# Two-layer graph network on one core: products of seven for the queries, one pass over the adjacency, softmax sums through DRAM

## The chip, the cores and the metric

The kernel runs on one core of a Trainium2 chip. The metric is the device time of one execution in microseconds (us). A core has five engines that work side by side, each on its own queue of instructions, in order: TensorE (PE, matrix products), VectorE (DVE), ScalarE (ACT), GpSimd (POOL) and SyncE (SP). SP and POOL also issue the DMA transfers here. An instruction that depends on another engine or on a transfer waits at the head of its queue, and what stands behind it waits too. SBUF is the on-chip memory of 128 partitions; PSUM holds the results of PE.

## The reference

The input is x (16 graphs, 1024 nodes, 256 channels) and one adjacency matrix of 1024 x 1024 that all graphs share. Two layers are computed, each with a layer norm before and the input added after.

```python
# layer 0
h = jnp.maximum(_layernorm(x), 0.0)          # per graph: fea = h transposed
c_adj = jnp.mean(fea, axis=1)                # one number per node
A = jnp.abs(jnp.abs(sigmoid(diff) - 0.5) - 0.5) * 2.0   # diff: c_adj of all pairs of nodes
Wg = adj * A_s                               # A_s: the symmetric mean of A
g = relu(einsum('bcn,bnm->bcm', fea, Wg) * para)        # the queries, 4 heads of 64
k, v = h @ kv_w
out = softmax(q k^T * scale) v               # attention over all 1024 nodes
# layer 1
A_norm = adj + I; deg = column sums + row sums - diagonal; dinv = rsqrt(deg)
agg = einsum('nm,bmd->bnd', A_norm * dinv[:, None] * dinv[None, :], h1)
out = bn(relu(bn(agg @ W1.T + b1)) @ W2.T + b2)         # bn: statistics over all nodes of all graphs
```

Everything is in 32-bit floats. Two things matter for the change. The weights Wg of the queries differ from graph to graph and have to be made anew for each. The matrix of the second layer is the same for all graphs and is scaled on both sides by dinv, the inverse root of the degrees.

## The kernel before

The first layer and the first product of the second run in `layers()`, graph after graph; the rest of the second layer (`second()`) follows once the statistics over all graphs are known. Profile lines written as L149 are line numbers of the kernel before.

**Attention.** `attention()` runs 256 steps: 16 graphs, two pairs of heads (k), two halves of 512 queries (f), four groups g of two node tiles. A step issues the scores of its group on PE (`sc`, L704), their exponentials on ACT (`p`, L712) and the additions of these on DVE (`acc`, L734), and then the product with the values of the step before (`o`, L745). After the four groups of a unit, `divide()` sums `acc` over the partitions with a product by ones (`sums`, L762). The result is 64 times repeated in each head's partitions, a tile of 128 x 512; DVE takes its reciprocal in four parts (`inv`, L771), multiplies `os` by it (L774), PE transposes (`ot`, L798) and DVE adds to x (L802). Two reductions (L777, L778) keep the extremes of `inv` in `seen` for a check at the end, which decides whether a slower variant of the kernel (`shifted`) has to run.

**Background.** PE is kept busy between scores by pieces of other work, each of eight matmuls of 512 columns. `background(b)` is a generator of these pieces, and a running sum of their costs (`due`, `done`) decides how many follow in each step. While graph b is in attention, its pieces are: the queries of graph b+1 (`queries`, `pg`, 16 pieces), the keys and values of b+1 (`keys_values`, `pk` and `pv`), the aggregation of b-1 over the adjacency (`aggregate`, `pa`, 14 pieces), the first linear product of b-1 (`hidden`, `py`), and the preparation of b+2. `weave` puts side work of the other engines between the pieces: `weigh` makes the weights `w` of the queries (ACT makes abs and tanh, L394 and L402; DVE multiplies by the loaded adjacency, L381), `Norm` makes the layer norms.

**Seven products.** `aggregate` already computes its 1024 x 1024 by 1024 x 256 product in the Strassen-Winograd way: the matrices are cut into quarters, seven products of quarters replace eight, and the quarters are combined by additions before and after. The combined quarters of the adjacency do not depend on the graph. `graph()` makes them once, during graph 1: it loads tiles `au`, scales them by the row `dbc` of dinv (L239), combines them on POOL (L246 to L249), and stores seven matrices in DRAM (`aht_d`, L251 to L253), from which SP loads pieces for each graph (`aht`). The degrees come before that, during graph 0: `degrees()` loads the transposed adjacency a first time (`at`), sums its rows on ACT, and takes the diagonal on DVE.

**Buffers.** Tiles come from pools that hand out their buffers in turn: a new tile waits until the last reader of the tile that had its buffer is done. `p4` has four buffers for each tag; the adjacency (`adj`, `at`, `au`, `aht`) shares one tag there, and `w` has another. `py` holds `y` and the small combined tiles. The order of the instructions on each engine is that in which the program issues them.

**The second layer.** `hidden` stores its results with POOL (`y_d`, L565). `second()` loads them again with SP (`yin_f`, L973), applies the statistics that POOL and DVE finish (`sm`, L82, L83, L917 to L919), combines the quarters of `w2` on POOL (L963 to L966) and multiplies (`m_f`, L1017).

Of the kernel before, what the change touches and what calls it, by code (L numbers as in the profile page):

```python
# [23 lines left out]
def gnn_two_layers_kernel(  # L24
# [36 lines left out]
    w2 = const.tile([P, HC, C], F32, name="w2")  # L61
# [4 lines left out]
    stats2 = const.tile([P, CC, B * NH, 6], F32, name="stats2")  # L66
# [6 lines left out]


# [10 lines left out]
    def layers(shifted):  # L85
# [12 lines left out]
        p3 = st.enter_context(tc.tile_pool(name=f"p3_{kind}", bufs=3))  # L98
        p4 = st.enter_context(tc.tile_pool(name=f"p4_{kind}", bufs=4))
# [41 lines left out]

        def bank(name):
            return ps_mm.tile([P, FB], F32, tag="mm", name=name)
# [15 lines left out]
        def load_adj(q, th, name):  # L159
            t = p4.tile([P, TH, FB], F32, tag="adj", name=name)  # L160
            nc.sync.dma_start(
                out=t,
                in_=adj[th * TH * P : (th + 1) * TH * P, q * FB : (q + 1) * FB].rearrange(
                    "(t p) m -> p t m", p=P
                ),
            )
            return t
# [4 lines left out]
        dbc = big.tile([P, N], F32, name="dbc")  # L172
        w1 = big.tile([P, CC, H1], F32, name="w1")
        rows = big.tile([P, NH, NT], F32, name="rows")

        def columns_of(col, name):

            cbs = []
            for g in range(NT // 4):
                cb = p2.tile([P, 4, P], F32, tag="cb", name=f"cb_{name}_{g}")  # L180
                nc.vector.tensor_copy(
                    cb, col[:, 4 * g : 4 * g + 4].unsqueeze(2).to_broadcast([P, 4, P])
                )
                cbs.append(cb)
            return cbs
# [9 lines left out]
        def load_adj_t(t, name):  # L195
            tile_ = p4.tile([P, N], F32, tag="adj", name=f"{name}_{t}")
# [3 lines left out]
        deg_sm = big.tile([P, 6, NT], F32, name="deg")  # L200
        row, diag, col, deg, tmp_deg, dinv = (deg_sm[:, i, :] for i in range(6))

        def degrees():

            nc.sync.dma_start(out=w1, in_=w1_t.rearrange("(k p) j -> p k j", p=P))
            nc.sync.dma_start(out=w2, in_=w2_t.rearrange("(k p) c -> p k c", p=P))
            nc.vector.tensor_reduce(row, rows.rearrange("p q t -> p t q"), AX.X, ALU.add)
            for t in range(NT):
                a = load_adj_t(t, "at")
                yield 0.0  # L210
                blk = a[:, t * P : (t + 1) * P]
                nc.scalar.activation(a, a, AF.Copy, accum_out=col[:, t : t + 1])
                db = p1.tile([P, P], F32, tag="db", name=f"db_{t}")
                nc.vector.tensor_mul(db, blk, ident)
                nc.vector.tensor_reduce(diag[:, t : t + 1], db, AX.X, ALU.add)
                yield 0.0
            nc.vector.tensor_add(deg, col, row)
            nc.vector.tensor_sub(deg, deg, diag)
            rsqrt(dinv, deg, 1.0, tmp_deg)

        def graph():


            HT, HB = NT // 2, FB // 2
            for t in range(HT):
                for part in range(2):
                    cols = slice(part * HB, (part + 1) * HB)
                    a = p4.tile([P, 2, NH, HB], F32, tag="adj", name=f"au_{t}_{part}")
# [6 lines left out]
                    for n in range(2):  # L235
                        if part == t * P // HB:
                            blk = a[:, n, n, t * P % HB : t * P % HB + P]
                            nc.vector.tensor_add(blk, blk, ident)
                        nc.vector.tensor_mul(  # L239
                            a[:, n], a[:, n], dbc.rearrange("p (m c) -> p m c", m=NH)[:, :, cols]  # L240
                        )
# [12 lines left out]
                    yield 0.0  # L254

# [107 lines left out]
        def weigh(b):  # L363
# [11 lines left out]
            for slot in range(2 * NH * NP + 1):  # L375
# [11 lines left out]
                if not odd and i < NH * NP:  # L387
# [3 lines left out]
                    w = p4.tile([P, TH, FB], F32, tag="w", name=f"w_{b}_{q}_{th}")  # L391
# [14 lines left out]

        def queries(b):

# [65 lines left out]
        def quarters(b):  # L474


            h = hs["b", b]
            HT = NT // 2
            return [h[:, n * HT : (n + 1) * HT, c * P : (c + 1) * P] for c in (0, 1) for n in (0, 1)]

        def combine(b):


            a11, a12, a21, a22 = quarters(b)
            s1s[b] = p1.tile([P, NT // 2, P], F32, tag="s1", name=f"s1_{b}")
            nc.vector.tensor_add(s1s[b], a21, a22)
            nc.vector.tensor_sub(a21, a11, a21)

        def aggregate(b):
# [5 lines left out]
            def load(upto):  # L495
                while len(pieces) <= min(upto, 7 * NP // 2 - 1):
                    i, th = divmod(len(pieces), NP // 2)
                    i = order[i]
                    a = p4.tile([P, TH, FB], F32, tag="adj", name=f"aht_{b}_{i}_{th}")
# [3 lines left out]
            load(2)  # L503
            yield 0.0
            a11, a12, a21, a22 = quarters(b)
            s1 = s1s[b]
# [4 lines left out]
            add, sub = nc.vector.tensor_add, nc.vector.tensor_sub  # L511

# [4 lines left out]
            def second(m):  # L517
                add(c11, m, c12)
                sub(a12, a12, a11)

            def fifth(m):
                add(c22, m, c21)
                add(c12, m, c12)

            for i, (left, after) in enumerate(
# [6 lines left out]
                    (a22, lambda m: add(c21, m, c21)),  # L532
                    (a12, lambda m: add(c12, m, c12)),
# [3 lines left out]
                for th in range(NP // 2):  # L537
                    n = i * NP // 2 + th
                    load(n + 3)
# [35 lines left out]
        def normed(b):  # L575
# [3 lines left out]
            combine(b)  # L579
# [4 lines left out]
        def normed_last():  # L584
# [6 lines left out]
            combine(B - 1)  # L591
            nc.gpsimd.dma_start(out=x1_d[B - 1], in_=xs[B - 1])

        def prepare(b, products):
# [8 lines left out]
            for k in range(CC):  # L603
                yield from weave(islice(products, 3), (0, islice(w, 3)))
# [7 lines left out]
        def background(b):  # L612

            nothing = iter(())
            if b == 0:
                yield from prepare(1, nothing)
                yield from weave(queries(1), (0, weighers[1]), (1, degrees()))
                cbs = columns_of(dinv, "deg")
                if B > 2:
                    load_x(2)  # L620
                    yield from weave(keys_values(1), (1, Norm(2, True).all()))
                else:
                    yield from keys_values(1)
# [3 lines left out]
                if B > 2:  # L627
                    yield from prepare(2, nothing)
# [3 lines left out]
            if b + 1 < B:  # L632
                whole = graph() if b == 1 else nothing
                yield from weave(queries(b + 1), (0, weighers[b + 1]), (0, whole))
                yield next(gather)
                yield from weave(keys_values(b + 1), (0, normed(b - 1)))
# [79 lines left out]
        class Unit:  # L716


            def __init__(self, b, k, f):
                self.at = (b, k, f)  # L720
                self.name = f"{b}_{k}_{f}"
                self.acc = None
                self.later = []
# [32 lines left out]
            def divide(self):  # L756

                b, k, f = self.at
                self.pt = ps_t.tile([P, FB], F32, tag="t", name=f"sums_{self.name}")
                for e in range(2):  # L760
                    r = slice(e * HD, (e + 1) * HD)
                    nc.tensor.matmul(  # L762
                        self.pt[r, :], ones, self.acc[:, e, :], start=True, stop=True
                    )
                self.inv = p1.tile([P, FB], F32, tag="inv", name=f"inv_{self.name}")
                u = (b * CC + k) * NH + f

                def invert(half):
                    for j in range(2 * half, 2 * half + 2):
                        c = slice(j * P, (j + 1) * P)  # L770
                        nc.vector.reciprocal(self.inv[:, c], self.pt[:, c])  # L771

                def scale():
                    nc.vector.tensor_mul(self.os, self.os, self.inv)  # L774

                def watch():
                    nc.vector.tensor_reduce(seen[:, 0, u : u + 1], self.inv, AX.X, ALU.max)  # L777
                    nc.vector.tensor_reduce(seen[:, 1, u : u + 1], self.inv, AX.X, ALU.min)  # L778

                invert(0)  # L780
                self.later = [lambda: invert(1), scale]
                self.watch = watch

            def behind_piece(self):
                if self.later:
                    self.later.pop(0)()

            def behind_pieces(self):
                while self.later:
                    self.behind_piece()  # L790

            def finish(self):
# [4 lines left out]
                for j in range(J):  # L797
                    nc.tensor.transpose(  # L798
                        pt[:, j * P : (j + 1) * P], self.os[:, j * P : (j + 1) * P], ident
                    )  # L800
                dst = xs[b][:, f * J : (f + 1) * J, k * P : (k + 1) * P]
                nc.vector.tensor_add(dst, pt.rearrange("p (j c) -> p j c", c=P), dst)  # L802
# [3 lines left out]
        def attention():  # L806
# [7 lines left out]
            for s in range(len(steps) + 2):  # L814
                if s < len(steps):
                    unit, g = steps[s]
                    b = unit.at[0]
                    if s % per_graph == 0:
# [3 lines left out]
                        total = 41.0 * (b + 1 < B) + 24.0 * (b > 0) + 6.0 * (b + 2 < B)  # L822
# [7 lines left out]
                finished = ended = None  # L830
                if pending and pending[0][1] <= s:
                    finished, _ = pending.pop(0)
                    finished.finish()
                if top:
                    done += advance(bg)
                    top = False
                if s < len(steps):
                    for pr in made:
                        unit.add(pr)
                if before is not None:  # L840
                    (last, g_last), prs = before
                    last.values(g_last, prs)
                    if g_last == NG - 1:
                        last.divide()
                        ended = last


                        pending.append((last, s + (2 if last.at[0] < B - 1 else 1)))
                while done < due and not top:
# [7 lines left out]
                    if ended is not None and cost > 1.0:  # L857
                        ended.behind_piece()
                if ended is not None:
                    ended.behind_pieces()  # L860
                if finished is not None:
                    finished.watch()
# [3 lines left out]
        with st:  # L866
            if shifted:
                for b in range(B):
# [7 lines left out]
                    run(weave(queries(b), (0, weighers[b])))  # L876
# [333 lines left out]
```

## Time and profile before

| | |
|---|---|
| median of 3 runs | 2698.32 us (2697.36 to 2698.34) |
| profiled execution, its own time | 2699.94 us |
| span of the profile | 2698.1 us |
| PE busy | 2620.7 us |
| DVE busy | 1742.3 us |
| ACT busy | 1292.3 us |
| POOL busy | 363.2 us |
| DMA | 355.05 MB, mean 132 GB/s |

Busy time counts what an engine executes, waits left out; matmuls overlap, so a busy PE says that the next matmul was there, not that the array was full. In the rows of groups, a form like `128x512 f32<-128x512 f32 x64 | 43.9, 686 | 3.3` gives the sizes, the count, the total busy time in us, the mean of one in ns, and the idle time just before, with the engine or transfer that ended it. A graph in the middle of the first layer takes 151 us.

### The profile page before, as it was taken

The page shows a single profiled execution, that of the slowest core. Times are in us where ns is not written, and L with a number is a line of the kernel's source. Part 1 is how long each engine was busy: PE and PEld are TensorE (multiplying, and loading weights), DVE is VectorE, ACT ScalarE, POOL GpSimd, SP SyncE. Part 2 cuts the span into 40 slices and gives each one's busy share as a digit, 9 for nine tenths or more (in the row PEclk, how much of TensorE's full clock was granted, in tenths as well). Part 3 has the DMA queues.
Part 4 walks back from the last instruction along what each step waited for, and adds up shares of the span by engine and source line. Part 5 has one row for each costly group of instructions (what it writes and reads, how often), then busy time and mean ns, then how long its engine had stood idle before and what let it go on. Part 6 is the DMA issues. An engine that isn't in the chain of part 4 may idle for free.

```text
span 2698.1 us, 32021 instructions
## 1 busy us (share of the span) xinstructions
PE 2620.7 (97%) x12106; PEld 968.3 (36%) x12106; DVE 1742.3 (65%) x2624; ACT 1292.3 (48%) x1845; POOL 363.2 (13%) x428
## 2 busy tenths in 40 slices
PE   7999999999999999999999999999999999989994
PEld 3333333333333333333333333333333333324443
DVE  5767666666666656666666666566666666656675
ACT  5653444536363544445363635444453634335544
POOL 0016000000000100000000001000000001026653
PEclk9999999999999999999999999999999999999997
DMA  4416414243332424142423324241424213355549
GB/s 156 159 58 225 161 53 164 86 148 103 107 116 98 141 80 158 51 168 83 150 100 109 114 98 141 84 155 51 168 82 152 99 63 118 113 215 187 202 182 364
DMA packets 128613, 355.05 MB, mean 132 GB/s; under 512 B 11969, under 2 KB 32961, under 8 KB 122305
## 3 DMA queue, kind: packets, MB, share of 16 engines
q1 hardware_dynamic: 109120, 278.44, 30.3%
q0 software_dynamic: 19328, 74.46, 7.3%
q8 instruction: 98, 1.61, 0.2%
q14 instruction: 67, 0.54, 0.1%
HBM read 278.41 MB, written 74.45 MB: 131 GB/s over the span
## 4 chain that ended last, share of the span: by engine, by line
PE 93%; DMA 3%; DVE 2%; issue 2%; ACT 1%; POOL 0%; SPq 0%; POOLq 0%; DVEq 0%; ACTq 0%
PE sc L704 18%; PE o L745 18%; PE pg L149 16%; PE pa L149 13%; PE py L149 7%; PE m_f L1017 7%; PE pk L149 4%; PE pv L149 4%; PE sums L762 2%; DMA out_dram<-xo_f 2%; PE ot L798 1%; PE htp L352 1%; PE cbp_c L192 1%; DMA y_d<-y 0%; DVE acc L734 0%
## 5 line engine op out<-in xcount | busy, mean ns | idle before, releaser
L712 ACT ACTIVATE p<-sc 128x1024 f32<-128x1024 f32 x512 | 496.4, 1021 | 700.8 <-PE sc L704 700.6
L734 DVE TENSOR_TENSOR acc<-acc,p 128x1024 f32<-128x1024 f32 x384 | 471.2, 1227 | 133.8 <-ACT p L712 112.5
L704 PE MATMUL sc<-q,k 64*128 64x512 f32 x2048 | 510.6, 617 | 0.5 <-ACT p L712 0.5
L745 PE MATMUL o<-p,v 128*64 128x512 f32 x2048 | 496.1, 605 | 0.0
L149 PE MATMUL pg<-w,h_a 128*64 128x512 f32 x2048 | 457.1, 596 | 7.5 <-DVE q L432 7.5
L149 PE MATMUL pa<-aht,h_b 128*64 128x512 f32 x1536 | 346.0, 592 | 2.7 <-DMA aht<-aht_d 2.7
L704 PEld LDWEIGHTS sc<-q,k 64*128 64x128 f32 x2048 | 176.6, 186 | 321.9 <-issue 270.3
L149 PEld LDWEIGHTS pg<-w,h_a 128*64 128x64 f32 x2048 | 148.2, 138 | 301.8 <-issue 281.7
L771 DVE RECIPROCAL inv<-sums 128x128 f32<-128x128 f32 x256 | 223.7, 921 | 24.6 <-PE sums L762 24.6
L149 PE MATMUL py<-at,w 128*64 128x512 f32 x1024 | 230.8, 592 | 2.1 <-ACT y L564 2.1
L745 PEld LDWEIGHTS o<-p,v 128*64 128x64 f32 x2048 | 124.3, 136 | 286.1 <-issue 285.9
L394 ACT ACTIVATE w<-cbc,csum 128x512 f32<-128x512 f32 x256 | 170.2, 714 | 74.3 <-PE pg L149 74.2
L731 DVE TENSOR_TENSOR acc<-p,p 128x1024 f32<-128x1024 f32 x64 | 78.5, 1226 | 194.8 <-ACT p L712 194.8
L381 DVE SCALAR_TENSOR_TENSOR w<-w,adj 128x1024 f32<-128x1024 f32 x128 | 156.5, 1223 | 54.7 <-ACT w L402 54.7
L149 PEld LDWEIGHTS pa<-aht,h_b 128*64 128x64 f32 x1536 | 110.6, 137 | 216.6 <-issue 204.9
L564 ACT ACTIVATE y<-py,vec 128x512 f32<-128x512 f32 x128 | 87.6, 684 | 188.4 <-PE py L149 155.1
L565 POOL DMA_DIRECT2D y_d<-y x128 | 70.7, 553 | 685.1 <-ACT y L564 681.9
L402 ACT ACTIVATE w<-w 128x1024 f32<-128x1024 f32 x128 | 134.8, 1053 | 1.7
L149 PEld LDWEIGHTS py<-at,w 128*64 128x64 f32 x1024 | 74.0, 137 | 147.8 <-issue 131.3
L149 PE MATMUL pv<-kvw,ht 128*64 128x256 f32 x1024 | 116.2, 379 | 0.4 <-DVE v L469 0.4
L82 POOL TENSOR_SCALAR lnsm_b<-mv_b 128x4 f32<-128x4 f32 x32 | 7.3, 230 | 805.2 <-DVE mv_b L277 805.1
L802 DVE TENSOR_TENSOR x<-ot,x 128x512 f32<-128x512 f32 x64 | 44.2, 691 | 110.6 <-PE ot L798 109.8
(133 smaller groups left out, 2526.4 us busy)
## 6 DMA issues: line engine op xcount, KB each, us to landing
aht<-aht_d SPq DMA_DIRECT2D x224, 512.0 KB, 4.2
adj<-in_adj_dram SPq DMA_DIRECT2D x128, 512.0 KB, 4.2
y_d<-y POOLq DMA_DIRECT2D x128, 256.0 KB, 2.8
yin_f<-y_d SPq DMA_DIRECT2D x32, 1024.0 KB, 6.3
x<-in_x_dram SPq DMA_DIRECT2D x32, 512.0 KB, 4.7
para<-in_para_dram SPq DMA_DIRECT2D x64, 256.0 KB, 4.1
x_d<-x POOLq DMA_DIRECT2D x16, 1024.0 KB, 4.2
xo_f<-x_d SPq DMA_DIRECT2D x32, 512.0 KB, 8.5
```

Of the source, the lines that this page charges most:

```text
L149: nc.tensor.matmul(dst[r], left[:, r], right, start=start, stop=stop)
L381: nc.vector.scalar_tensor_tensor(w, w, 1.0, a, op0=ALU.add, op1=ALU.mult)
L394: nc.scalar.activation(w[:, t, :], cbc[:, q * FB : (q + 1) * FB], AF.Abs, bias=csum[:, th * TH + t : th * TH + t + 1], scale=-1.0,)
L402: nc.scalar.activation(made[i], made[i], AF.Tanh, scale=-0.5 / C)
L564: nc.scalar.activation(y, made, AF.Identity, bias=b1[:, j : j + 1])
L704: nc.tensor.matmul(sc[:, e, :], ks[b][k][r, m * P : (m + 1) * P], qs[b][k][r, f * FB : (f + 1) * FB], start=True, stop=True,)
L712: nc.scalar.activation(pr, sc, AF.Exp)
L731: nc.vector.tensor_add(self.acc, self.held, pr)
L734: nc.vector.tensor_add(self.acc, self.acc, pr)
L745: nc.tensor.matmul(self.o[r, :], vs[b][k][:, m, r], pr[:, e, :], start=(m == 0), stop=(m == NT - 1),)
L771: nc.vector.reciprocal(self.inv[:, c], self.pt[:, c])
L1017: nc.tensor.matmul(made, left[:, j, :], right[:, j, :], start=(j == 0), stop=(j == JH - 1))
```

## The change

- From graph 2 on, `queries` uses seven products of quarters, 14 pieces instead of 16. Left operands are quarters of h, right operands quarters of the weights, which DVE turns into differences (`take`) in place; nine additions from PSUM put the four results together. Graphs 0 and 1 keep the old form, now `plain_queries`. Eight buffers hold `w` (pool `p8`, which `aggregate`'s loads share, five ahead instead of three).
- `degrees()` and `graph()` become one pass during graph 0: each `au` tile is loaded once, summed on ACT, its diagonal taken on DVE, combined on POOL without the scale and stored. `aggregate` multiplies its results by `dbc` instead (`scale`). The tiles of the adjacency have three buffers instead of four.
- The sums of exponentials: `sums()` copies the product by ones from PSUM (ACT), writes one row of each head to DRAM, and reads it back transposed as 128 x 8 (three DMAs on POOL). `add_output()` takes the reciprocal of this small tile and applies it after the transposes. The unit is finished two steps after its last group, in the last graph too, except for the last two units.
- The keys of b+1 come before its queries, the norm of b-1 begins within the queries, x of graph 2 is loaded earlier.
- `w2` is loaded, and `stats2` allocated, in the pools of the second layer.

The diff, cut to its core:

```diff
-    w2 = const.tile([P, HC, C], F32, name="w2")
+    sums_d = [dram.tile([2, FB], F32, name=f"sums_d{u}") for u in range(B * CC * NH)]
+        p8 = st.enter_context(tc.tile_pool(name=f"p8_{kind}", bufs=8))
+        def double(slots):
+            for _ in slots:
+                next(slots, None)
+                yield 0.0
...
-            t = p4.tile([P, TH, FB], F32, tag="adj", name=name)
+            t = p3.tile([P, TH, FB], F32, tag="adj", name=name)
...
-            nc.sync.dma_start(out=w2, in_=w2_t.rearrange("(k p) c -> p k c", p=P))
...
-                    a = p4.tile([P, 2, NH, HB], F32, tag="adj", name=f"au_{t}_{part}")
+                    a = p3.tile([P, 2, NH, HB], F32, tag="adj", name=f"au_{kind}_{t}_{part}")
...
+                        u = t + n * HT
+                        nc.scalar.activation(
+                            a[:, n], a[:, n], AF.Copy, accum_out=sums[:, u : u + 1]
+                        )
                         if part == t * P // HB:
                             blk = a[:, n, n, t * P % HB : t * P % HB + P]
+                            db = py.tile([P, P], F32, tag="y", name=f"db_{u}")
+                            nc.vector.tensor_mul(db, blk, ident)
+                            nc.vector.tensor_reduce(diag[:, u : u + 1], db, AX.X, ALU.add)
                             nc.vector.tensor_add(blk, blk, ident)
-                        nc.vector.tensor_mul(
-                            a[:, n], a[:, n], dbc.rearrange("p (m c) -> p m c", m=NH)[:, :, cols]
-                        )
...
+        def combine(tag, b, engine):
+            a11, a12, a21, a22 = quarters(tag, b)
+            s1s[tag, b] = p1.tile([P, NT // 2, P], F32, tag="s1", name=f"s1_{tag}_{b}")
+            engine.tensor_add(s1s[tag, b], a21, a22)
+            engine.tensor_sub(a21, a11, a21)
+
         def queries(b):
+            combine("a", b, nc.vector)
...
+            def finish(k, q):
+                dst = qs[b][k][:, q * FB : (q + 1) * FB]
+                nc.vector.tensor_mul(dst, dst, paras[k, q])
+                soon(lambda: nc.scalar.activation(dst, dst, AF.Relu, scale=SCALE))
...
+            def take(i, x, y, part):
+                nc.vector.tensor_sub(block(i)[part], block(x)[part], block(y)[part])
+            def first(m):
+                nc.scalar.copy(c12, m)
+                nc.scalar.copy(c21, m)
+                nc.vector.tensor_sub(a11, s1, a11)
...
+            def sixth(m):
+                for c in (c12, c22, c21):
+                    add(c, m, c)
...
+                    (a11, 0, (), first),
+                    (a12, 1, ((0, 2, 0, 0), (0, 2, 0, 1)), second),
+                    (s1, 0, (), third),
+                    (a12, 3, ((2, 3, 2, 1), (0, 3, 0, 0)), fourth),
+                    (a21, 2, ((0, 3, 0, 1), (1, 1, 0, 0)), fifth),
+                    (a11, 0, ((1, 1, 0, 1),), sixth),
+                    (a22, 1, (), seventh),
...
-                    a = p4.tile([P, TH, FB], F32, tag="adj", name=f"aht_{b}_{i}_{th}")
+                    a = p8.tile([P, TH, FB], F32, tag="w", name=f"aht_{b}_{i}_{th}")
...
-            load(2)
+            load(4)
...
+            def scale(c, g):
+                nc.vector.tensor_mul(c, c, dbc[:, g * FB : (g + 1) * FB])
...
-                whole = graph() if b == 1 else nothing
-                yield from weave(queries(b + 1), (0, weighers[b + 1]), (0, whole))
+                w, products, norm = weighers[b + 1], keys_values(b + 1), normed(b - 1)
+                yield from weave(islice(products, 4), (0, islice(w, 4)))
+                yield from weave(queries(b + 1), (0, double(w)), (9, islice(norm, 5)))
                 yield next(gather)
-                yield from weave(keys_values(b + 1), (0, normed(b - 1)))
+                yield from weave(products, (0, norm))
...
-            def divide(self):
+            def sums(self):
...
+                row = py.tile([P, FB], F32, tag="y", name=f"row_{self.name}")
+                nc.scalar.copy(row, pt)
+                nc.gpsimd.dma_start(
+                    out=sums_d[u], in_=row.rearrange("(e r) c -> e r c", r=HD)[:, 0, :]
+                )
+                self.inv = p2.tile([P, FB // P, 2], F32, tag="inv", name=f"inv_{self.name}")
+                for e in range(2):
+                    nc.gpsimd.dma_start(
+                        out=self.inv[:, :, e], in_=sums_d[u][e].rearrange("(j q) -> q j", q=P)
                     )
...
+            def add_output(self):
...
+                nc.vector.reciprocal(self.inv, self.inv)
+                nc.vector.tensor_mul(
+                    self.os.rearrange("p (j e c) -> p j e c", j=J, e=2),
+                    pt.rearrange("p (j e c) -> p j e c", j=J, e=2),
+                    self.inv.unsqueeze(3).to_broadcast([P, J, 2, HD]),
+                )
...
-                        total = 41.0 * (b + 1 < B) + 24.0 * (b > 0) + 6.0 * (b + 2 < B)
+                        total = (37.6 if b > 0 else 41.0) * (b + 1 < B) + 24.0 * (b > 0) + 6.0 * (b + 2 < B)
...
-                        pending.append((last, s + (2 if last.at[0] < B - 1 else 1)))
+                        pending.append((last, s + (2 if last.index < UNITS - 2 else 1)))
...
         with st:
+            w2 = wp.tile([P, HC, C], F32, name="w2")
+            nc.sync.dma_start(out=w2, in_=w2_t.rearrange("(k p) c -> p k c", p=P))
```

## The prediction

> **What bounds the kernel now.** I read the shares of busy time first, then the chain of waits, the windows by graph, PE's waits, and last the timeline at the three places where PE stands still.
>
> ```profile
> PE 2620.7 (97%) x12106; PEld 968.3 (36%) x12106; DVE 1742.3 (65%) x2624; ACT 1292.3 (48%) x1845; POOL 363.2 (13%) x428
> PE 93%; DMA 3%; DVE 2%; issue 2%; ACT 1%; POOL 0%; SPq 0%; POOLq 0%; DVEq 0%; ACTq 0%
> ```
>
> PE carries 93% of the chain and is idle for 77 us in all. The next view shows where: columns are window, length, then busy us and count of PE, PEld, DVE, ACT and POOL, clock, DMA share and GB/s.
>
> ```profile
> 60.00:210.00 150.00, 143.24 (x682) 52.87 (x678) 101.76 (x146) 95.03 (x135) 18.60 (x21) 0.98 0.33 113
> 210.00:360.00 150.00, 145.05 (x682) 51.14 (x684) 106.78 (x159) 67.94 (x100) 45.82 (x59) 0.97 0.51 173
> 360.00:511.00 151.00, 151.00 (x725) 53.66 (x722) 97.20 (x145) 72.50 (x105) 10.07 (x17) 1.00 0.33 112
> 511.00:662.00 151.00, 151.00 (x730) 54.04 (x730) 97.37 (x146) 73.81 (x107) 10.06 (x17) 1.00 0.34 113
> ```
>
> A middle graph is 151 us of PE without a gap, with DVE at 64%: a PE instruction less is worth its whole duration there, until another engine is late. Only the stages of graphs 0 and 1 have gaps (6.8 and 5.0 us). PE's waits, with total us, times and longest, name them:
>
> ```profile
> PE pg L149 <- DVE q L432: 7.5, 3, 4.7
> PE m_f L1017 <- POOL sm L83: 4.8, 1, 4.8
> PE pa L149 <- DMA aht<-aht_d: 2.7, 2, 1.5
> ```
>
> The timeline of graph 1 shows the first of them:
>
> ```profile
> 208.71 0.29 DVE L238 TENSOR_TENSOR au<-au,ident 128x128 f32<-128x128 f32 x1 [3.32 <-DMA au<-in_adj_t_dram]
> 213.29 3.68 PE L149 MATMUL pg<-w,h_a 128*64 128x512 f32 x8 [4.72 <-DVE q L432]
> 218.63 3.45 PE L149 MATMUL pg<-w,h_a 128*64 128x512 f32 x8 [1.66 <-DVE q L432]
> ```
>
> DVE stood at an adjacency tile that had not landed; behind it in DVE's order were q (L432) and the weights (L381), and PE waited for them. The eight matmuls then took 3.68 and 3.45 us instead of 1.89.
>
> [...]
>
> **The change, part by part.**
>
> *Queries as seven products.* Sixteen pieces of eight matmuls become fourteen. Pieces of pa and py follow each other at 1.72 us (2350.77, then 2352.49). Two pieces less are 3.44 us a graph; graphs 2 to 15 make 14: -48.2 us, all on PE's path.
>
> *DVE's load.* A graph adds 8 subtractions of weights at 1.23 us (as L734), 13 additions of 512 columns at 0.69 and 4 scalings of the aggregate at 0.69: 9.8 + 9.0 + 2.8 = 21.6 us. It loses 16 reciprocals at 0.92 and 8 reductions at 0.67, and gains 4 reciprocals and 8 reductions over 8 elements[...]: -14.7 - 5.4 + 2.0 = -18.1. So DVE goes from 97.4 to 101 us of some 148. The mean is safe; the placing is not. The subtractions and additions all fall in the first half of a graph's steps, where DVE also multiplies weights (L381, 1.23) and adds exponentials (up to 2.5 us a step). Adding each step's instructions up, the two fullest have 9.9 and 10.1 us of DVE against 9.5 and 8.9 of PE; the fullest before has 8.7 of 11.5. Laying them out in order by hand, two places come late: the first piece of the third product waits for the difference w_0-w_2, which stands behind acc and so behind exp (0.6 us, 0.6 to 1.4), and the third piece of v waits for copies in DVE's backlog (0.45, 0 to 2.1). 1.05 x 14 = +15 us (0, if the order is kinder, to +35).
>
> *Sums of exponentials.* Each unit gets on ACT a copy (0.59) and on POOL three DMAs: a 4 KB row to DRAM and two reads of 512 four-byte elements, which must wait for the row. No row shows these. Low end: y_d's landing twice, 0.6 + 2.8 + 2.8 = 6.2 us; high end: the landing of aht_d stores of short pieces, 4.4, plus two issues at 0.8 and another 6.3, the median of 1 MB loads: 13.1. I take 8.5. The reader comes two steps later, about 16 us, so I cost it at 0; if it came later than that, DVE would stop at the reciprocal with acc and q behind it. POOL's y_d stores queue behind the row's landing wait (about 3 us); y has four buffers and a new one is due each 1.7 us or slower, so they hold.
>
> *Aggregate's loads.* SP issues the same 14 loads a graph, five ahead instead of three, in eight buffers shared with w. They wait for w's last readers, done before; the 2.7 us of pa's waits at the end may vanish. The last unit's sums now take the DRAM trip before the last Norm; eight py pieces (13.7 us) stand beside it, and its h_b comes about 2 us late. Together 0 (-2.7 to +4).
>
> *Keys first, norm woven earlier, load_x(2) earlier.* The same four pk pieces, the same BN, POOL and ACT operations; x's loads on SP and x1_d's store on POOL keep their number. The cover is PE's own backlog: 0; before graph 0, 1 MB of x ahead of adjacency loads on SP's queue could cost up to 3 us.
>
> *Degrees and combinations in one pass.* Removed: eight 512 KB loads and 16 multiplications L239 (13.9 us of DVE) with graph 1's two stops; with the slowed clock, graphs 0 and 1 lose up to 17 us of gaps. Added in graph 0: eight tiles, each two 256 KB loads on SP (4.0 us to landing), two ACT sums (1.6), DVE's diagonal (1.5, every second), four POOL subtractions (L246 to L249 now average 0.84 to 1.19, 4.3 a tile; alone 0.72, as L963, so 2.9) and three POOL stores, of which the first frees the tile (4.4). A tile holds its buffer 13 to 15 us. There are three buffers, not four, taken in turn, and graph 1's adjacency loads take turns too: the third au tile falls into the buffer of the first and second. Its ACT sums stand ahead of exp in ACT's order, so PE waits for exp. By hand, PE stops for about 3.7, 15, 5.4, 2.7 and 8 us. I take 30 of these 35, since some subtractions will run uncontended, and 5 for the clock after long stops: +35 - 17 = +18 us (-10, if the tiles come in time, to +40).
>
> *w2's load at the start of the second layer.* In before, w2 was long there and the yin loads left early; POOL's sm set the start:
>
> ```profile
> 2401.12 2.01 SPq L973 DMA_DIRECT2D yin_f<-y_d  x4
> 2418.93 0.54 POOL L565 DMA_DIRECT2D y_d<-y  x1 [0.68 <-ACT y L564]
> 2422.17 3.75 PE L1017 MATMUL m_f<-yin_f,w 128*128 128x512 f32 x4 [4.84 <-POOL sm L83]
> ```
>
> Now w2 takes memory that y's last stores still read: its DMA waits for their landing (2418.93 + 2.7 = 2421.6), and the yin loads stand behind it on SP. 0.5 MB and 1 MB land some 6 us later; relu 0.8: 2428.5, or +6.3. Against that, no yin loads slow the last y stores (ACT waited for those landings, PE for ACT, 2.1 us). +5 us (+1 to +11).
>
> Sum: -48.2 + 15 + 18 + 5 = -10 us. The profiled execution took 2699.9 us (span 2698.1 plus 1.8), so 2690; the median of the runs lies 1.6 under it: 2688 us.
>
> **The rivals.** *All cover holds:* DVE's backlog drains in the steps with 2.7 us of ACT work, and the tiles land in time: -48 + 0 - 5 + 3 = -50, 2648. For it: DVE at 69%. Against: the two steps with more DVE than PE. *Graph 0's chain decides and the change is slower:* ACT stops at each au tile for the whole life of the tile before. At 45 us of stops (landings of 6.3, the slow end of the au loads) and 25 in the middle graphs: -48 + 25 + 33 + 6 = +16, 2714. It decides once the stops together pass 48 us; for it speaks that before's easier chain, without POOL, already has gaps. *The DRAM trip is late:* beyond 16 us each us can cost PE one in each of the 64 units; one us late, -10 + 64 = +54, 2752. Against it speak the 2.8 us of y_d. *The seven products reach only graphs 2 to 15*, as the order of the built program shows, so the change cannot miss altogether.
>
> **How the numbers follow.** My sum's case, 2666 to 2702: 0.44. All hidden, 2640 to 2666: 0.22. Slower by the chain or the middle queue, 2702 to 2730: 0.27. The late trip or worse: 0.07. The range 2648 to 2724 leaves out under 2 in 10. A measurement tells about 0.2%, 5.4 us: faster means under 2692.9. From the cases: 0.22 + 0.28 faster, 0.15 same, 0.35 slower.
>
> **What would show it.** Windows of a middle graph of 148 to 149 us with 1 us of PE idle, at pg and pv behind DVE; 147.5 without idle means all hidden, over 150 the queue. In graph 0, ACT waiting for DMA au and sc or o for exp, 30 us. At the start of layer two, the first m_f after a DMA wait. A PE idle at ot or acc behind DVE's reciprocal would mean the trip is late. A time under 2640 or over 2730 would prove the working wrong.

## The result, and the profile after

The changed kernel takes 2703.8 us (median of 4 runs, 2700.74 to 2704.51) against 2697.84 for the kernel before in the same session. The ratio is 1.0021, 95% interval 1.0003 to 1.0038: slower by about 0.2%, where the forecast was 10 us faster. The time lies inside the range, on the other side of no change. The profiled execution has a span of 2702.7 us, 4.6 more than before; this difference is what is taken apart here. The four runs of the changed kernel span 3.8 us and the profiled one is the slowest of them, so 2 or 3 us of the whole can be those of one execution.

The shares of busy time and the chain of waits, after:

```profile
PE 2580.4 (95%) x11882; PEld 955.1 (35%) x11882; DVE 1741.5 (64%) x2775; ACT 1338.3 (50%) x1953; POOL 546.7 (20%) x620
PE 79%; DVE 7%; ACT 4%; DMA 4%; issue 3%; POOL 2%; SPq 0%; POOLq 0%; DVEq 0%; ACTq 0%
```

PE has 224 matmuls less, as the seven products promise, and is busy 40 us less. The time isn't shorter because PE now stands still: it carries 79% of the chain instead of 93%. DVE's total has not changed at all (1741.5 against 1742.3 us).

The windows from the first exponential of a graph to that of the next say where. First the kernel before, graphs 0, 1 and 7; then the kernel after, the same graphs (window, length, busy us and count of PE, PEld, DVE, ACT and POOL, clock, DMA share, GB/s):

```profile
63.24:182.05 118.81, 113.48 (x554) 43.50 (x552) 83.19 (x125) 78.12 (x116) 4.44 (x6) 0.98 0.32 106
182.05:341.49 159.44, 153.05 (x714) 53.42 (x714) 112.45 (x167) 71.42 (x104) 59.52 (x73) 0.96 0.53 179
1082.82:1231.09 148.27, 148.27 (x714) 52.90 (x712) 95.38 (x144) 71.20 (x104) 10.07 (x18) 1.00 0.34 114
```

```profile
66.11:216.46 150.35, 119.58 (x554) 44.23 (x552) 76.08 (x123) 81.31 (x134) 58.05 (x71) 0.90 0.36 116
216.47:363.25 146.78, 145.27 (x698) 51.93 (x696) 99.52 (x159) 74.08 (x109) 21.88 (x28) 1.00 0.34 117
1097.18:1243.96 146.78, 145.27 (x698) 51.91 (x696) 98.19 (x157) 74.09 (x109) 22.41 (x30) 1.00 0.35 115
```

Graph 0 grew by 31.5 us, while graph 1 shrank by 12.7. PE is idle for 30.8 us in graph 0, against 5.3 before, and its 554 matmuls take 6.1 us more there, at a mean granted clock of 0.90 against 0.98. A middle graph became 1.5 us shorter, though two pieces of PE (3.44 us) went. Its PE now has 1.5 us of gaps. (It takes 148.27 us before, not the 151 us given further up, which was the length of the windows read there.) Over the whole span, from one kernel to the other:

| stretch | before, us | after, us | difference |
|---|---|---|---|
| start to the first exponential | 63.2 | 66.1 | +2.9 |
| graph 0 | 118.8 | 150.4 | +31.5 |
| graph 1 | 159.4 | 146.8 | -12.7 |
| graphs 2 to 13, each | 148.27 | 146.79 | -1.48 (together -17.8) |
| graphs 14, 15 up to the second layer | 301.5 | 297.3 | -4.2 |
| second layer | 276.0 | 280.7 | +4.8 |

The second layer is the stretch that varies most: in the six kernels of the experiments that edit nothing in it, it takes 277.8 to 280.7 us.

PE's waits name the causes (what waited, for what; total us, times, longest):

```profile
PE sc L825 <- ACT p L833: 27.3, 5, 14.0
PE m_f L1130 <- ACT yin_f L1092: 11.3, 1, 11.3
PE pv L155 <- DVE v L582: 10.7, 14, 0.8
PE pg L155 <- DVE w L455: 9.3, 13, 0.7
PE pg L155 <- ACT k L565: 2.9, 2, 2.1
```

Before, sc waited for exp once (0.5 us), pv for v once (0.4), and the first m_f for POOL's scale (4.8); the other two pairs are new. The waits for q (7.5 us, then 3.4) and aht (2.7, then none) shrank or went.

### The profile page after: what moved, and what is told of

It is laid out like the page before. It is cut to its first block, busy times and chain, and to the rows that moved or that the text cites. A ratio compares the mean times of both kernels' runs of the same rounds, so it can differ in the third digit from the quotient of the medians.

```text
span 2702.7 us, 32228 instructions
## 1 busy us (share of the span) xinstructions
PE 2580.4 (95%) x11882; PEld 955.1 (35%) x11882; DVE 1741.5 (64%) x2775; ACT 1338.3 (50%) x1953; POOL 546.7 (20%) x620
## 4 chain that ended last, share of the span: by engine, by line
PE 79%; DVE 7%; ACT 4%; DMA 4%; issue 3%; POOL 2%; SPq 0%; POOLq 0%; DVEq 0%; ACTq 0%
PE sc L825 16%; PE o L866 16%; PE pa L155 13%; PE pg L155 9%; PE py L155 8%; PE m_f L1130 7%; PE pk L155 4%; PE pv L155 2%; PE sums L883 2%; DMA out_dram<-xo_f 2%; DVE acc L855 2%; ACT w L393 1%; PE htp L351 1%; ACT w L401 1%; DVE q L482 1%
## 5 line engine op out<-in xcount | busy, mean ns | idle before, releaser
L825 PE MATMUL sc<-q,k 64*128 64x512 f32 x2048 | 514.3, 621 | 27.3 <-ACT p L833 27.3
L155 PE MATMUL pg<-w,h_a 128*64 128x512 f32 x1600 | 358.1, 593 | 6.3 <-DVE q L545 3.4
L886 POOL DMA_DIRECT2D sums_d<-row x64 | 37.3, 582 | 1051.8 <-ACT row L885 1051.8
L155 PEld LDWEIGHTS pg<-w,h_a 128*64 128x64 f32 x1600 | 115.4, 137 | 234.8 <-issue 213.7
L455 DVE TENSOR_TENSOR w<-w,w 128x1024 f32<-128x1024 f32 x112 | 131.5, 1214 | 0.0
L155 PE MATMUL pv<-kvw,ht 128*64 128x256 f32 x1024 | 119.2, 380 | 10.7 <-DVE v L582 10.7
L891 POOL DMA_DIRECT2D inv<-sums_d x128 | 98.1, 770 | 135.0 <-DMA sums_d<-row 90.5
```

The costliest lines, as they stand in the source:

```text
L155: nc.tensor.matmul(dst[r], left[:, r], right, start=start, stop=stop)
L455: nc.vector.tensor_sub(block(i)[part], block(x)[part], block(y)[part])
L825: nc.tensor.matmul(sc[:, e, :], ks[b][k][r, m * P : (m + 1) * P], qs[b][k][r, f * FB : (f + 1) * FB], start=True, stop=True,)
L891: nc.gpsimd.dma_start(out=self.inv[:, :, e], in_=sums_d[u][e].rearrange("(j q) -> q j", q=P))
```

## The experiments

Each one edits one thing in the changed kernel, so its time is to be read against 2703.8 us and its span against 2702.7.

**The seven products, undone.**

```diff
-                yield from weave(queries(b + 1), (0, double(w)), (9, islice(norm, 5)))
+                yield from weave(plain_queries(b + 1), (0, double(w)), (9, islice(norm, 5)))
...
-                        total = (37.6 if b > 0 else 41.0) * (b + 1 < B) + 24.0 * (b > 0) + 6.0 * (b + 2 < B)
+                        total = 41.0 * (b + 1 < B) + 24.0 * (b > 0) + 6.0 * (b + 2 < B)
```

> All graphs take the queries as sixteen pieces, everything else as changed. Theory: a middle graph loses the wait for the weights' difference (0.72 us and its restart) and gains two pieces, 3.43 us; with the wait for v kept it is 149.3 us, without it 148.3, so the whole is 2724 to 2738. Rival: DVE's queue is what sets a middle graph, the seven products buy nothing, and the graph stays at 146.8 to 147.3 us, the whole at 2704 to 2711.

It took 2725.44 us, ratio to before 1.0102 (1.0073 to 1.0132). Its window of graph 7:

```profile
1106.14:1254.40 148.26, 148.26 (x714) 52.93 (x712) 81.40 (x136) 73.06 (x107) 19.88 (x30) 1.00 0.34 114
```

This is the 148.27 us of before, without a gap: both waits come with the seven products, and all the rest of the change costs a middle graph nothing. DVE has 81.4 us here against 95.4 before, so the new sums, less the scaling, freed 14 us, and the seven products took 16.8 back. They still pay, 1.48 us a graph, but not 3.44. Graph 1 too is 148.27 us here, so taking the adjacency's pass out of it was worth 159.44 - 148.27 = 11.2 us.

**The first subtraction of weights, earlier.**

```diff
             def first(m):
...
                 nc.vector.tensor_sub(a11, s1, a11)
+                take(0, 2, 0, 0)
...
-                    (a12, 1, ((0, 2, 0, 0), (0, 2, 0, 1)), second),
+                    (a12, 1, ((0, 2, 0, 1),), second),
```

> The first of the subtractions of weights is issued behind the first product instead of one piece later. Theory: pg's wait of 0.72 us falls away because DVE does it ahead of the additions that wait for exp; a middle graph goes from 146.79 to 145.9 us, the whole to 2691. Rival: DVE is full there, the additions move back and the wait returns at the next difference or at v, and the graph stays above 146.5.

The wait is seen in the timeline of the changed kernel in graph 7. DVE takes acc when exp has come, and the two differences of w after it, though nothing they need was late:

```profile
1118.45 1.92 ACT L833 ACTIVATE p<-sc 128x1024 f32<-128x1024 f32 x2
1119.00 3.60 PE L155 MATMUL pg<-w,h_a 128*64 128x512 f32 x16
1119.49 2.56 DVE L855 TENSOR_TENSOR acc<-acc,p 128x1024 f32<-128x1024 f32 x2 [0.59 <-ACT p L833]
1121.96 2.35 DVE L455 TENSOR_TENSOR w<-w,w 128x1024 f32<-128x1024 f32 x2
1123.33 1.94 PE L155 MATMUL pg<-w,s_a 128*64 128x512 f32 x8 [0.72 <-DVE w L455]
```

With the edit, the first of them stands ahead of acc, in the same graph:

```profile
1110.54 1.22 DVE L455 TENSOR_TENSOR w<-w,w 128x1024 f32<-128x1024 f32 x1
1114.59 2.54 DVE L856 TENSOR_TENSOR acc<-acc,p 128x1024 f32<-128x1024 f32 x2
1117.52 1.89 PE L155 MATMUL pg<-w,s_a 128*64 128x512 f32 x8
```

The kernel took 2690.4 us, ratio to before 0.9968 (0.9959 to 0.9978). Each middle graph takes 145.85 us and the wait for w is gone; that for v stays as it was. The gain is 0.94 us a graph for a wait of 0.72. The rows show where the other 0.22 us are. The 16 matmuls of pg ahead of these begin at 1114.09 here and take 3.60 us, so the next piece begins 0.17 us before their shown end; a wait is counted only from that end on. And the eight matmuls behind the wait took 1.94 us, against 1.89 here.

**The values copied by ACT.**

```diff
-                    nc.vector.tensor_copy(
+                    nc.scalar.copy(
                         vs[b][k][:, 2 * g : 2 * g + 2, :], pv[:, :, k * P : (k + 1) * P]
                     )
```

> ACT instead of DVE copies the values from PSUM. Theory: pv's wait of 0.79 us and its restart are DVE's queue alone, and fall away; a middle graph goes from 146.79 to 145.8 us, the whole to 2690. Rival: ACT's copies stand behind exp and the norm's relu, and the wait comes back at pv or at sc: above 146.5 us a graph, 2700 or more.

The third piece of v needs a PSUM bank that the first one's copies free, and these stood behind the same kind of backlog:

```profile
1157.13 3.62 PE L155 MATMUL pv<-kvw,ht 128*64 128x256 f32 x32
1157.59 2.54 DVE L855 TENSOR_TENSOR acc<-acc,p 128x1024 f32<-128x1024 f32 x2
1160.04 0.69 DVE L441 TENSOR_TENSOR q<-q,para 128x512 f32<-128x512 f32 x1
1160.65 1.41 DVE L582 COPY v<-pv 128x256 f32<-128x256 f32 x4
1161.54 1.73 PE L155 MATMUL pv<-kvw,ht 128*64 128x256 f32 x14 [0.79 <-DVE v L582]
```

It took 2687.43 us, ratio to before 0.996 (0.9945 to 0.9976), a middle graph 145.78 us. The theory holds: 1.01 us a graph for a wait of 0.79. The start became 2.3 us shorter as well, which neither theory had; there too the wait of pv for v (0.42 us) and one of two of pg for q (1.7 us) went. Of the 16.4 us, 13.1 are the 13 graphs and 2.3 the start; the second layer was 2.6 us shorter, and nothing in it was edited. What moved in the start was not taken apart.

**The sums of exponentials, as before.** The unit's functions of the kernel before are put back, with the reciprocal written over `acc`:

```diff
-                self.inv = p2.tile([P, FB // P, 2], F32, tag="inv", name=f"inv_{self.name}")
+                self.inv = self.acc[:, 0, :]
...
+                def invert(half):
+                    for j in range(2 * half, 2 * half + 2):
+                        c = slice(j * P, (j + 1) * P)
+                        nc.vector.reciprocal(self.inv[:, c], self.pt[:, c])
```

> The sums of exponentials as before (reciprocals and extremes over 128x512 on DVE, no trip through DRAM), with the seven products and all else as changed; the reciprocal is written over the sums of exponentials, for want of memory. Theory: DVE carries 18 us more a graph, and the steps of the queries, already fuller on DVE than on PE, fall behind by up to 4 us: a middle graph takes 148.5 to 151 us, the whole 2727 to 2765. Rival: there is room in the other steps, and the graph stays at 146.8 to 147.5, the whole under 2715; then the new sums bought nothing.

It took 2712.48 us, ratio to before 1.0055 (1.0035 to 1.0075). The window of graph 7 and its waits:

```profile
1101.70:1249.28 147.58, 145.27 (x698) 51.88 (x696) 114.08 (x169) 71.86 (x105) 12.95 (x18) 1.00 0.33 115
```

```profile
PE pv L155 <- DVE v L582: 21.0, 14, 1.6
PE pg L155 <- DVE w L455: 9.8, 13, 1.1
```

The theory's size fell: 16 us more of DVE in a graph (114.1 against 98.2) cost PE only 0.8, nearly all at the copies of v (21.0 against 10.7 us). The whole lost 8.7 us by it; the 13 graphs alone, at 0.8 us, make about 10, and the second layer was 2.7 us shorter than in the profile of the changed kernel. So adding the load of each step overstates a queue: here what stood in the queue cost only where PE asked for its end.

**The au tiles in other buffers.**

```diff
-                    a = p3.tile([P, 2, NH, HB], F32, tag="adj", name=f"au_{kind}_{t}_{part}")
+                    a = p8.tile([P, 2, NH, HB], F32, tag="w", name=f"au_{kind}_{t}_{part}")
```

> The au tiles of graph 0 come from the eight buffers of the weights, so that they no longer take turns with the adjacency loads in three buffers. Theory: the 30 us of PE's gaps in graph 0 come from the reuse of a buffer whose store has not landed; graph 0 shrinks from 150.4 to about 122 us, with 3 to 8 us of gaps, and the whole to about 2677 us. Rival: the stops come from the tiles' own loads and from the sums on ACT ahead of exp; then graph 0 stays above 143 us and the whole above 2697.

The changed kernel's timeline in graph 0, first SP's loads of the tiles, then ACT's sums and PE:

```profile
99.77 1.21 SPq L222 DMA_DIRECT2D au_f<-in_adj_t_dram  x2
111.18 1.21 SPq L222 DMA_DIRECT2D au_f<-in_adj_t_dram  x2
123.83 1.20 SPq L222 DMA_DIRECT2D au_f<-in_adj_t_dram  x2
```

```profile
114.38 0.63 ACT L228 ACTIVATE au_f<-au_f 128x512 f32<-128x512 f32 x1 [6.18 <-DMA au_f<-in_adj_t_dram]
115.45 0.63 ACT L228 ACTIVATE au_f<-au_f 128x512 f32<-128x512 f32 x1 [0.35 <-DMA au_f<-in_adj_t_dram]
117.24 1.91 ACT L833 ACTIVATE p<-sc 128x1024 f32<-128x1024 f32 x2
118.30 3.78 PE L825 MATMUL sc<-q,k 64*128 64x512 f32 x8 [14.02 <-ACT p L833]
```

A tile is loaded each 11.4 to 12.7 us, when the one that had its buffer has been stored (between 100 and 165 us SP's loads waited five times for a store of `aht_d` from `au_f`, 51.5 us in all); ACT's sums wait for the load, exp for the sums, and PE for exp. With the eight buffers the kernel took 2677.37 us, ratio to before 0.9924 (0.9895 to 0.9953). Graph 0 takes 124.3 us with 10.2 idle (expected were 3 to 8), and the waits of sc for exp go from 27.3 to 6.8 us. Whether a fourth buffer of its old kind would have done as much wasn't tried.

**w2 apart.**

```diff
+        w2p = st.enter_context(tc.tile_pool(name=f"w2p_{kind}", bufs=1))
...
-            w2 = wp.tile([P, HC, C], F32, name="w2")
+            w2 = w2p.tile([P, HC, C], F32, name="w2")
...
-            stats2 = wp.tile([P, CC, B * NH, 6], F32, name="stats2")
+            stats2 = w2p.tile([P, CC, B * NH, 6], F32, name="stats2")
```

> w2 and the second layer's statistics lie in a pool behind the others, over memory that attention left long before. Theory: w2's load no longer waits for the last stores of y, the loads of yin leave with it some 15 us earlier, and the gap of 11.3 us before the first product of the second layer goes to about 5 (POOL's and DVE's scale, as before); the whole is about 2697. Rival: the transfers then slow the last stores as in the kernel before, PE's wait for y returns, and only 2 to 4 us are won, 2700 to 2702.

The changed kernel at the handover: the last y leaves at 2411.70, w2 waits for it to land, and yin and PE for w2.

```profile
2411.70 0.54 POOL L676 DMA_DIRECT2D y_d<-y  x1 [1.18 <-ACT y L675]
2414.17 0.38 SPq L1063 DMA_DIRECT2D w<-in_w_t_dram  x1
2414.61 23.46 SPq L1086 DMA_DIRECT2D yin_f<-y_d  x6
2421.98 3.75 PE L1130 MATMUL m_f<-yin_f,w 128*128 128x512 f32 x4 [11.30 <-ACT yin_f L1092]
```

Apart, the loads of yin leave at 2384.19, and the gap before m_f is 4.1 us:

```profile
2384.19 1.95 SPq L1087 DMA_DIRECT2D yin_f<-y_d  x4
2414.89 3.78 PE L1131 MATMUL m_f<-yin_f,w 128*128 128x512 f32 x4 [4.13 <-ACT yin_f L1093]
```

It took 2693.98 us, ratio to before 0.9984 (0.9974 to 0.9994): 9.8 us won, 7.2 of them at the gap. The second layer was 2.2 us shorter too, and that is not shown to be w2's doing: 0.7 us are a wait of m_f for t_f that went, but with w2 left where it was, four other experiments (the seven products undone, the values by ACT, the old sums, x later) had one of 277.8 to 278.5 us, where this had 278.5. The rival, slow last stores of y, didn't come: with y's eight stores 1.7 us apart, PE never waited for one.

**x of graph 2, later.**

```diff
-                load_x(2)
                 run(weave(plain_queries(0), (0, weighers[0]), (5, Norm(1, True).all())))
...
             if b == 0:
+                load_x(2)
                 differences_1 = columns_of(csums[1], "c1")
```

> x of graph 2 is loaded at the start of graph 0's background instead of ahead of its queries. Theory: its 1 MB stood ahead of the adjacency loads of graph 0, and the start goes back from 66.1 to 63.3 us, the whole to 2701. Rival: the start is longer for another reason (three buffers for the adjacency instead of four), and stays at 66.

It took 2700.27 us, ratio to before 1.001 (1.0001 to 1.002); the start went from 66.1 to 63.95 us. Most of the 2.9 us were this load.

**All five at once.**

> All five at once: au in the weights' buffers, w2 and its statistics apart, the first subtraction earlier, v copied by ACT, x of graph 2 later. Theory: the causes are separate and add up: 2703.8 - 26.4 - 9.8 - 13.4 - 13.5 - 2.9 = 2638, a middle graph 144.9 us without a gap. Rival: the stops share their cover, and one of them comes back where another goes: 2650 to 2665.

It took 2640.27 us, ratio to before 0.9788 (0.9772 to 0.9805): 58 us faster than the kernel before. Graph 7 in its windows:

```profile
1056.12:1200.94 144.82, 144.82 (x698) 51.76 (x696) 95.32 (x149) 76.28 (x117) 22.39 (x30) 1.00 0.34 117
```

148.27 - 144.83 = 3.44 us: the whole of the two pieces. The causes are separate and add up to within 3 us of the sum that was expected. The gains measured one by one come to 69.5 us, 6 more than the 63.5 won together: the copies of v and the later load shorten the same start (2.3 and 2.2 us alone, 3.3 together), and the rest lies in the second layer.

## Why the prediction was wrong

*The gain on PE*: right. 3.44 us a graph, shown bare by all five edits together, and in graph 14 of the changed kernel, which had no wait and lost 3.42.

*DVE's load*: right in the mean. It said 101 us a graph; 98.2 were measured, because it started from a window of 151 us, longer than a graph (the rise is 2.8 us where 3.5 were taken). For the same reason its windows of 148 to 149 us for a middle graph were too long: 148.27 - 3.44 + 1.05 is 145.9. The 2.0 us for the 4 reciprocals and 8 reductions over 8 elements were its estimate. Before's profile has two DVE operations over 128x8 at 157 and 167 ns (L217, L218), which for 12 makes 1.9 to 2.0 us; measured were 193 ns for a reciprocal and about 150 for a reduction, 2.0 us together. It named both places that came late, the difference w_0-w_2 and the third piece of v.

*What the two waits cost*: this is the step that failed, the 1.05 us a graph. The waits are 0.72 and 0.79 us, where 0.6 and 0.45 were taken, and each costs 0.22 us beyond the idle time shown (0.94 for 0.72, 1.01 for 0.79), for which the prediction had no term. Of the 0.91 us by which a graph was underestimated, 0.44 are these two, 0.34 the third piece of v and 0.12 the difference of w. Together 146.79 - 144.83 = 1.96 us, in the 13 graphs that have them: 25.5 us instead of 15. The stated bounds, up to 35, held it.

*Graphs 0 and 1*: right. Taken were 30 us of stops and 5 of slowed clock, less 17 of before's gaps: +18. PE had 30.8 us idle in graph 0 and was busy 6.1 longer, of which 5.5 went with the stops when the au tiles had other buffers; before's gaps and slowed clock were 5.3 in graph 0 and 11.2 in graph 1, which the pass left: 30.8 + 6.1 - 5.3 - 11.2 = +20.4. The order of the stops was right too: one of 14.0, then 4.2, 1.2 and 7.5.

*The start*: put at 0, up to 3, and it was 2.9, of which 2.2 are the load of x for graph 2.

*The handover*: taken at +5, with the tail at 0. Measured from graph 15 on: -0.8 before m_f and +4.8 after, +4.0. The gap grew from 4.8 to 11.3 us, about as taken (6.3), while the tail ahead of it became 7.2 us shorter: its waits for aht, y and os, 6.2 us together, are gone. Only y's 2.1 had been taken. The second layer's own +4.8 had no term. 2.2 of it come after PE's last matmul, which takes 29.1 us before, 29.2 with the old sums and 31.0 to 31.5 in all eight kernels with the sums' trip; why is open. 2.0 are its first eight matmuls: after the stop of 11.3 us they were started over 8.0 us, all at a granted clock of 0.50, where before, after 4.8 us, it was 6.0, the first 4.6 us of that at 0.50; but it was 6.2 after nearly equal stops in three of the experiments. That the handover came out near +5 is luck: two parts that were not foreseen cancel.

*The sums' trip*: right that PE never waits for it, and cheaper than taken (but for the 2.2 us at the end, which only the kernels with the trip show). In graph 7 the row's store was issued at 1139.77, the reads at 1141.91, and they landed 2.6 us after their issue: about 6.4 us from the copy, near the low end. The reading of 512 four-byte elements cost 0.77 us of issue. The reciprocal waited for its data three times in the whole run, 6.1 us on DVE, and PE never waited for it.

The sum with what was measured: -48.2 + 25.5 + 20.4 + 2.9 + 4.0 = +4.6 us, which is the difference of the spans. The miss of 15 us is 10.5 of middle waits, 2.9 of start and 2.4 of graph 0, less 1 at the end. Of the rivals, the one in which graph 0 and the queue decide came nearest: what was added, 25.5 + 20.4 + 2.9 + 4.0 = 52.8 us, passed the 48.2 that were saved. Its 25 us for the middle graphs were right; its 33 for graph 0 and 6 for the handover were too much.

## What to carry to other kernels

When work goes from an engine that never waits to one that is two thirds busy, look for the first consumer on the full engine of each thing that the other now makes, and count every wait with what it costs beyond the idle time shown (0.22 us here) and with the number of times that it recurs; a mean load says nothing of it. An instruction that waits for another engine belongs behind those that are ready and wanted: moving one subtraction ahead of an addition that waits for exp was worth 12 us (13 graphs of 0.94), and it cost nothing. A load put into buffers that something else must first store, or into memory whose last reader is a late store, brings that store's landing into the path of all that is queued behind it (27.3 us of PE's waits for exp, nearly all in graph 0, and 11.3 before m_f, which fell to 6.8 and 4.1 with other buffers), so choose the buffers by who frees them.

## What the runs showed of the hardware

A short wait of PE cost 0.22 us more than the idle time in its row: 0.94 for 0.72 in 13 graphs, 1.01 for 0.79 in 12, each to 0.01 us. In the first case 0.17 of it is that without the wait the next matmul starts before the shown end of the last.

After the longer stops PE ran slower. After stops of 4.17, 7.47 and 14.02 us in the changed kernel, of 5.42 with all five edits and of 3.58 with x later, eight scores took 3.78 to 3.79 us instead of 2.04, which they took after 1.21 us. In the kernel before, eight transposes (`htp`) took 1.97 us after a stop of 3.52, instead of 1.09 as in graph 2. After 2.07 us eight matmuls of pg took 1.94 us, no more than after a wait of 0.72.

The granted clock, read in windows of 0.1 to 0.5 us, goes with it: it was 0.50 while the slow scores and transposes ran, and 1.00 after the stops of 0.72, 1.21 and 2.07 us. It fell while PE stood still, 2.5 us after the last matmul in the stop of 4.17 us, 2.7 in that of 14.02, 3.7 in that of 11.30 before the second layer and 5.1 in that of 7.47. How long the slow stretch lasted differs: from PE's restart the clock stayed at 0.50 for 5.1, 5.7, 9.4 and 4.4 us in these four. Within such a stretch a short stop was followed by slow matmuls too: in the kernel before, pg's eight after 1.66 us took 3.45 us, the clock being at 0.50 since the stop of 4.72 ahead of it. After stops of 10.8 to 11.3 us before the second layer, its first eight matmuls were started over 6.2 us in three kernels and over 8.0 in four.

The strided read of 512 four-byte elements (2 KB) landed in 2.6 us, as quickly as y_d's 256 KB (2.6), and the row of 4 KB that it reads in 1.7.
